# Mamba's first load by itself, and the sum of x and its norm on ScalarE instead of GpSimd

## The chip, the cores and the metric

The kernel runs on one core of a Trainium2 chip. The core has five engines that run their own instruction queues side by side: TensorE (PE) for matrix products, VectorE (DVE), ScalarE (ACT), GpSimd (POOL), and SyncE (SP), which here only issues transfers. PE, DVE, ACT and POOL wait for one another through semaphores. The metric is the device time of one launch in microseconds, as the median of several runs. One further execution is recorded by the profiler; its own time is a little different from the median, and both are given below.

## The reference, cut to what matters

The input `x` has 4 sequences of 1024 tokens with 256 features, all in float32. Four blocks follow one another:

```python
x = x + lora_attention(layernorm(x))
x = x + moe_ffn(layernorm(x))          # best 1 of 4 experts, weighted by its probability
h = layernorm(x)
x = x + (h + mamba2(h))                # the block that the change touches
x = x + moe_ffn(layernorm(x))          # same weights as the first FFN
```

The third block is the one to keep in mind. It needs `h` twice: as the input of Mamba's projections, and in the sum `x + h`, to which Mamba's result is added at the end. The norm has no learned scale or offset, so `h = x * rstd + shift`, with `rstd` one over the root of a token's variance (plus 1e-5) and `shift = -mean * rstd`, both one number per token.

Inside `mamba2`, a projection makes a gate `z` (512 features), the convolved part `xBC` (512 + 128 + 128) and eight step sizes `dt`. `xBC` passes through a causal convolution over 4 tokens and a SiLU; the state-space part runs over chunks of tokens; its result is gated, normed and projected back to 256 features.

## The kernel before, in words

Three phases follow one another in time. Attention, with some tiles of the first FFN woven in, ends near 1200 us; the other tiles of the first FFN end near 1406 us; Mamba runs from there to about 2110 us with tiles of the second FFN woven in; the tiles that remain of the second FFN end the run. The output of the first FFN lies in HBM as `x_mid`.

Mamba is cut into eight `Half` objects of 512 tokens each, `halves[0]` to `halves[7]`: first the first halves of the four sequences (`g == 0`), then the second ones (`g == 1`). A half has these steps, whose lines the profile names:

- `fetch` (L1195) loads its 512 x 256 tokens, 512 KB, into `xs`, of which there are three buffers. Half 0 is fetched on ACT's queue, half 1 on SP's, and half n + 2 on SP's at the end of half n's turn.
- `front` is a generator of 14 steps. The first is the norm in `layernorm`: statistics (L169, L172), `rstd` (L173 and `rsqrt`, L149 to L154), `shift` (L178), all on DVE, then four ACT activations (L180) that write `xln`. The second step transposes `xln` on PE (L190), copies the result to `xT` on ACT (L139), and adds `xln` to `xs` on POOL through `in_parts` (L1178, called at L1207). The third makes the step sizes (`softplus`, L1160 on). Six steps `channels(cc)` follow (L1210 to L1237), in the order 4, 5, 0, 1, 2, 3; then four gates (L1243), and the sums of step sizes.
- `channels` multiplies on PE (L1219), takes the last three tokens of the half before from `carry` into the head of the buffer `raw` on POOL (L1223), copies the product behind them on ACT (L1224), saves the last three tokens into `carry` on POOL when `g == 0` (L1226), makes the first tap on ACT (L1228), the three other taps on DVE (L1232), the tanh on ACT into `raw` (L1235), and the SiLU on DVE (L1236). `raw` has two buffers, so a channel waits for L1236 of the one two before it.
- `prepare(i)` and `chunk(i)` do the state-space part of 128 tokens: masks and decays (L1318 to L1325, with products on POOL), transposes of the channels (L1335 to L1348), and the state.
- `back` is a generator of eight steps: four of `project`, which writes x + h + Mamba's result to `rows` (L1409, L1410), then the FFN's norm, its transposes, the routing (L252 on), and last the ranks (L277 on) with four scattering DMAs that POOL issues (L310) into `sorted_rows`.
- The tiles of the second FFN start with `ffn_some`: a table made on DVE (L345 to L379), then on SP's queue the gather of the first tile's rows (L426) and its weights (L443, L450). A tile begins on PE with the transposes of these rows (L461).

What sets the order is `plan`, a table of four tuples per half: "f" is a step of the next half's front, "b" a step of the back of the half before, "t" a step of FFN tiles, "s" the start of new tiles, and a number that chunk of the present half. An engine's instructions follow from the order in which the program issues them, as priorities, but a planner that estimates when operands are ready may let an instruction pass another of its engine; `keep_in_program_order` pins an instruction behind the one that the program issued last on that engine. Only the first statistic of each norm in Mamba is pinned.

Of the kernel before, what the change touches and what calls it, by code (L numbers as in the profile page):

```python
# [38 lines left out]
AF = mybir.ActivationFunctionType  # L39
ALU = mybir.AluOpType  # L40
AX = mybir.AxisListType

P = 128
# [7 lines left out]
DIN, DST, DCONV, NMH, HD = 512, 128, 4, 8, 64  # L51
# [3 lines left out]
TB = 512  # L55
# [23 lines left out]
def hybrid_block(ctx: ExitStack, tc: tile.TileContext, t, out: bass.AP):  # L79
    nc = tc.nc  # L80
# [12 lines left out]
    def ps1(name):  # L93
        return psum_now["pool"].tile([P, 512], F32, tag="one", name=name, bufs=psum_now["one"])
# [48 lines left out]
    def rsqrt(v, name):  # L143

        n = v.shape[1]
        bits = keep.tile([P, n], I32, tag=f"rs_bits{n}", name=f"rs_bits_{name}", bufs=2)
        y = bits.bitcast(F32)
        u = keep.tile([P, n], F32, tag=f"rs_u{n}", name=f"rs_u_{name}", bufs=2)
        nc.vector.tensor_single_scalar(bits, v.bitcast(I32), 1, op=ALU.logical_shift_right)  # L149
        nc.vector.tensor_scalar(bits, bits, -1.0, float(0x5F3759DF), op0=ALU.mult, op1=ALU.add)  # L150
        for i in range(3):
            nc.vector.tensor_tensor(u, y, y, ALU.mult)
            nc.vector.scalar_tensor_tensor(u, u, -0.5, v, op0=ALU.mult, op1=ALU.mult)
            nc.vector.scalar_tensor_tensor(v if i == 2 else y, u, 1.5, y, op0=ALU.add, op1=ALU.mult)  # L154
# [6 lines left out]
    def layernorm(pool, xs, xln, name, pinned=False, beside=None):  # L161

        n = xs.shape[1]
        stats = pool.tile([P, n, 6], F32, tag="ln_stats", name=f"stats_{name}", bufs=2)
        mv = pool.tile([P, n, 2], F32, tag="ln_mv", name=f"mv_{name}", bufs=2)
        both = pool.tile([P, n + 4 * (beside is not None)], F32, tag=f"ln_rstd{beside is not None}", name=f"rstd_{name}", bufs=2)
        rstd = both[:, 0:n]
        for i in range(n):
            first = nc.vector.bn_stats(stats[:, i, :], xs[:, i, :])  # L169
            if pinned and i == 0:  # L170
                tc.keep_in_program_order(first)
            nc.vector.bn_aggr(mv[:, i, :], stats[:, i, :])  # L172
        nc.vector.tensor_single_scalar(rstd, mv[:, :, 1], EPS, op=ALU.add)  # L173
        if beside is not None:
            nc.vector.tensor_scalar(both[:, n:], beside, 1.0 / DIN, EPS, op0=ALU.mult, op1=ALU.add)
        rsqrt(both, name)
        shift = pool.tile([P, n], F32, tag="ln_shift", name=f"shift_{name}", bufs=2)
        nc.vector.scalar_tensor_tensor(shift, mv[:, :, 0], -1.0, rstd, op0=ALU.mult, op1=ALU.mult)  # L178
        for i in range(n):
            nc.scalar.activation(  # L180
                xln[:, i, :], xs[:, i, :], AF.Identity, bias=shift[:, i : i + 1], scale=rstd[:, i : i + 1]
            )
        return both[:, n:]

    def transposed(xln, dst, name):

        for k in range(2):
            pt = ps1(f"xT_{name}_{k}")
            for i in range(4):
                nc.tensor.transpose(pt[:, i * P : (i + 1) * P], xln[:, i, k * P : (k + 1) * P], ident)  # L190
            evacuate(k, dst[:, k, :], pt)
# [3 lines left out]
    x_mid = tc.dram_tile([NTOK, D], F32, name="x_mid")  # L195
# [26 lines left out]
    def small(shape, tag, name, dtype=F32, bufs=2):  # L222
        return keep.tile([P, *shape], dtype, tag=tag, name=f"{tag}_{name}", bufs=bufs)
# [18 lines left out]
    def send_parts(rows, tok0, name):  # L242
        xln = rows[:, :, 0:D]
        layernorm(keep, rows[:, :, D : 2 * D], xln, f"f{name}")
        yield
        xT = small([2, TB], "xT_r", name, bufs=1)
# [265 lines left out]
    def full_tiles(n, size=FT):  # L512

        return max(0, -(-(n - NE * (size - 1)) // size))
# [586 lines left out]
    pb = ctx.enter_context(tc.tile_pool(name="phase_b", bufs=1))  # L1101
    rows_from.update(pool=pb, bufs=1)

    def work(name, tag, bufs):
        return pb.tile([P, 512], F32, tag=tag, name=name, bufs=bufs)
# [69 lines left out]
    def in_parts(n, size, operands, op):  # L1175

        for i in range(0, n, size):
            nc.gpsimd.tensor_tensor(*operands(slice(i, i + size)), op)  # L1178
# [4 lines left out]
    class Half:  # L1183
# [8 lines left out]
        def fetch(self, queue=nc.sync):  # L1192
            name = self.name
            self.xs = pb.tile([P, 4, D], F32, tag="xs", name=f"xs_{name}", bufs=3)
            queue.dma_start(self.xs, x_mid[self.tok0 : self.tok0 + TB, :].rearrange("(n p) d -> p n d", p=P))  # L1195

        def load(self, past):
            name = self.name
            xln = pb.tile([P, 4, D], F32, tag="xln", name=f"xln_{name}")
            if past:  # L1200
                past.rstd = layernorm(pb, self.xs, xln, name, pinned=True, beside=past.sumsq)
            else:
                layernorm(pb, self.xs, xln, name, pinned=True)
            yield
            self.xT = pb.tile([P, 2, TB], F32, tag="xT_b", name=f"xT_{name}")
            transposed(xln, self.xT, name)
            in_parts(4, 1, lambda i: (self.xs[:, i], self.xs[:, i], xln[:, i]), ALU.add)  # L1207
            yield

        def channels(self, cc):  # L1210

            name = f"{self.name}_{cc}"
            if cc == 4 and self.g == 0:
                carries[self.b] = pb.tile([P, NCC, DCONV - 1], F32, tag="carry", name=f"carry_{self.b}", bufs=NB)
                nc.gpsimd.memset(carries[self.b], 0.0)
            carry = carries[self.b]
            pp = ps1(f"xbc_{name}")
            for k in range(2):
                nc.tensor.matmul(  # L1219
                    pp, w_in[:, k, DIN + cc * P : DIN + (cc + 1) * P], self.xT[:, k, :], start=(k == 0), stop=(k == 1)  # L1220
                )
            raw = pb.tile([P, DCONV - 1 + TB], F32, tag="xbc", name=f"raw_{name}", bufs=2)
            nc.gpsimd.tensor_copy(raw[:, 0 : DCONV - 1], carry[:, cc, :])  # L1223
            nc.scalar.copy(raw[:, DCONV - 1 :], pp)  # L1224
            if self.g == 0:
                nc.gpsimd.tensor_copy(carry[:, cc, :], raw[:, TB:])  # L1226
            acc = work(f"xc_{name}", "xc", 12)
            nc.scalar.activation(  # L1228
                acc, pp, AF.Identity, bias=conv_b[:, cc : cc + 1], scale=conv_w[:, cc, DCONV - 1 : DCONV]
            )  # L1230
            for k in range(DCONV - 1):
                nc.vector.scalar_tensor_tensor(  # L1232
                    acc, raw[:, k : k + TB], conv_w[:, cc, k : k + 1], acc, op0=ALU.mult, op1=ALU.add
                )
            nc.scalar.activation(raw[:, 0:TB], acc, AF.Tanh)  # L1235
            nc.vector.scalar_tensor_tensor(acc, raw[:, 0:TB], 1.0, acc, op0=ALU.add, op1=ALU.mult)  # L1236
            self.xc.append(acc)  # L1237
# [199 lines left out]
    halves = [Half(b, g) for g in range(2) for b in range(NB)]  # L1437
    evacuates.update(only_act=True)

    halves[0].fetch(nc.scalar)  # L1440
    halves[1].fetch()
    for _ in halves[0].front():
        pass
    halves[0].prepare(0)

    plan = (
        ("f", "b", "t", "b", "t", 0, "b", "t", "b", "t"),
        ("b", "f", "t", "f", "t", 1, "t", "f", "b", "f", "t"),
        ("b", "t", "f", "f", "t", 2, "f", "f", "b", "s", "t"),
        ("t", "f", "f", "t", "f", 3, "t", "f", "f"),  # L1450
    )
    y_out = out.rearrange("b s d -> (b s) d")
# [2 lines left out]
    for n, H in enumerate(halves):  # L1455
        after = halves[n + 1] if n + 1 < len(halves) else None
        front = after.front(halves[n - 1] if n else None) if after else iter(())
        for i in range(4):
            if i < 3:
                H.prepare(i + 1)  # L1460
            for step in plan[i]:
                if step == i:
                    H.chunk(i)
                elif step == "s":

                    n_tiles = full_tiles(n * TB, P) - n_done
                    n_done += n_tiles
                    if n_tiles:
                        coming = ffn_some(n_tiles, y_out, f"f2_{n}", 0 if after else n_tiles - 1)
                        next(coming)  # L1470
                else:
                    next({"b": back, "f": front, "t": tiles}[step], None)
            if i == 3 and after:
                after.prepare(0)

        if n + 2 < len(halves):
            halves[n + 2].fetch()
        tiles, back = chain(tiles, coming), H.back()
        coming = iter(())

# [70 lines left out]
```

## Time and profile before

| what | value |
|---|---|
| median of three runs | 2311.2 us (2309.44 to 2313.97) |
| profiled execution | 2317.05 us, its span 2315.3 us |
| mean granted TensorE clock | 0.949 of full speed |
| busy: PE, DVE, ACT, POOL | 2110.2, 1378.8, 867.1, 844.3 us |
| first loads of Mamba issued | 1410.05 us |
| first matmul of Mamba | 1421.42 us |
| POOL, adds of `xln` to `xs` (L1178) | 32 of 739 ns, 22.8 us in all |
| POOL, copies of three tokens (L1223, L1226) | 48 of 450 ns and 24 of 393 ns |
| ACT, activations of the same size as an add (L180) | 32 of 589 ns |

"Busy" is the time in which an engine executes something, over the whole span. The view by groups gives for each line of the code the number of instructions, the busy time, the mean of one, and the time that the engine stood idle before them with what ended it ("<-"). The timeline gives the start of each instruction or run of like instructions, its time, and in brackets the idle time before it. Durations and places all come from the one profiled execution.

### The profile page before, as it was taken

What the parts mean: (1) busy time and instruction counts of PE and PEld (TensorE: products, weight loads), DVE (VectorE), ACT (ScalarE), POOL (GpSimd) and SP (SyncE); (2) the same over time, 40 slices, a digit from 0 to 9 for tenths busy, and PEclk for the clock granted to TensorE, in tenths of its full rate; (3) what the DMA queues carried; (4) which work ended last, traced back from release to release, by engine and by line L of the source; (5) the groups of instructions that cost most, each with busy time, mean ns of one, the idle gap of its engine ahead of it and who ended that gap; (6) DMA issues with size and microseconds to landing.
All of it is one profiled execution on the core that took longest, in us unless ns stands there. A gap on an engine that the chain in (4) does not pass through costs nothing. (4 is left out here: it accounts for less than half of the span.)

```text
span 2315.3 us, 34722 instructions
## 1 busy us (share of the span) xinstructions
PE 2110.2 (91%) x12322; PEld 1472.2 (64%) x12322; DVE 1378.8 (60%) x3470; ACT 867.1 (37%) x1709; POOL 844.3 (36%) x1455
## 2 busy tenths in 40 slices
PE   5899999999999998989988997898799999999997
PEld 4444454554545555655566994566487877879987
DVE  5666666556655545565344334787967777775522
ACT  3365644445444443443411112453433433332210
POOL 3344433344443242341121111665635353443221
PEclk8799998999989999999999997899899999999999
DMA  9101011300131212132245683002153453544788
GB/s 332 36 21 50 22 36 51 102 29 24 40 121 67 86 44 81 35 115 87 88 164 186 221 320 108 0 10 89 65 204 136 138 194 125 181 162 142 273 317 304
DMA packets 148977, 278.19 MB, mean 120 GB/s; under 512 B 19965, under 2 KB 92031, under 8 KB 148801
## 3 DMA queue, kind: packets, MB, share of 16 engines
q1 hardware_dynamic: 120240, 227.45, 28.7%
q0 software_dynamic: 9920, 30.25, 3.6%
q10 hardware_dynamic: 18640, 18.23, 2.5%
q8 instruction: 100, 1.64, 0.3%
q14 instruction: 77, 0.62, 0.1%
HBM read 225.17 MB, written 51.12 MB: 119 GB/s over the span
## 5 line engine op out<-in xcount | busy, mean ns | idle before, releaser
L873 DVE TENSOR_REDUCE mx<-s 128x2 f32<-128x1024 f32 (+3 forms) x384 | 363.8, 953 | 86.6 <-PE s L864 80.6
L908 ACT ACTIVATE pe<-s 128x1024 f32<-128x1024 f32 (+3 forms) x384 | 309.0, 811 | 252.1 <-PE s L900 196.1
L919 PE MATMUL acc<-pe,v 128*32 128x512 f32 (+3 forms) x1536 | 263.1, 514 | 13.7 <-POOL pe L911 11.9
L911 POOL TENSOR_SCALAR_AFFINE_SELECT pe<-pe 128x256 f32<-128x256 f32 x256 | 104.4, 409 | 445.8 <-ACT pe L908 445.5
L476 PE MATMUL gu_f<-t_xT_f,t_Wg_f 128*128 128x128 f32 (+1 forms) x1216 | 236.1, 317 | 3.1 <-DVE t_xT_f L141 2.3
L476 PE MATMUL gu_f<-t_xT_f,t_Wu_f 128*128 128x128 f32 (+1 forms) x1216 | 229.9, 312 | 0.2
L872 DVE TENSOR_TENSOR s<-s,amats 128x256 f32<-128x256 f32 x256 | 109.2, 428 | 155.3 <-PE s L864 114.0
L476 PEld LDWEIGHTS gu_f<-t_xT_f,t_Wg_f 128*128 128x128 f32 x1216 | 183.3, 193 | 24.8 <-issue 6.4
L492 PE MATMUL y_f<-t_Wd_f,t_h_f 128*128 128x256 f32 x816 | 187.4, 383 | 7.6 <-DVE t_rows_f L499 2.8
L864 PE MATMUL s<-ks,qs 64*128 64x512 f32 (+3 forms) x768 | 172.8, 401 | 23.3 <-ACT pe L908 12.3
L476 PEld LDWEIGHTS gu_f<-t_xT_f,t_Wu_f 128*128 128x128 f32 x1216 | 184.9, 192 | 12.0 <-DMA t_Wu_f<-in_Wu 1.0
L900 PE MATMUL s<-qs,ks 64*128 64x512 f32 (+3 forms) x768 | 182.9, 441 | 10.0 <-DVE mx L873 7.4
L900 PEld LDWEIGHTS s<-qs,ks 64*128 64x128 f32 x768 | 80.0, 189 | 170.3 <-issue 95.4
L159 DVE SCALAR_TENSOR_TENSOR t_h_f<-t_h_f,gu_f 128x512 f32<-128x512 f32 x102 | 69.9, 686 | 193.5 <-ACT t_h_f L158 193.5
L492 PEld LDWEIGHTS y_f<-t_Wd_f,t_h_f 128*128 128x128 f32 x816 | 152.6, 191 | 38.0 <-issue 6.2
L158 ACT ACTIVATE t_h_f<-gu_f 128x512 f32<-128x512 f32 x102 | 60.9, 597 | 280.2 <-PE gu_f L476 280.1
L900 PE MATMUL s<-mneg,sel_r 64*128 64x512 f32 (+3 forms) x768 | 161.6, 367 | 0.0
L864 PEld LDWEIGHTS s<-ks,qs 64*128 64x128 f32 x768 | 85.0, 195 | 74.1 <-ACT pe L908 25.3
L1232 DVE SCALAR_TENSOR_TENSOR xc_m<-raw_m,conv_w,xc_m 128x512 f32<-128x512 f32 x144 | 111.4, 784 | 16.8 <-ACT xc_m L1228 14.9
L1178 POOL TENSOR_TENSOR m_m<-m_m,gm_m 128x256 f32<-128x256 f32 x128 | 93.8, 764 | 63.7 <-ACT gm_m L1325 62.7
L787 PE MATMUL qkv<-weff,xT 128*128 128x192 f32 x512 | 108.0, 357 | 7.7 <-ACT ks L838 4.3
L787 PEld LDWEIGHTS qkv<-weff,xT 128*128 128x128 f32 x512 | 87.8, 202 | 28.6 <-ACT ks L838 10.3
(450 smaller groups left out, 3912.9 us busy)
## 6 DMA issues: line engine op xcount, KB each, us to landing
t_Wg_f<-in_Wg SPq DMA_DIRECT2D x38, 1024.0 KB
t_Wu_f<-in_Wu SPq DMA_DIRECT2D x38, 1024.0 KB
t_Wd_f<-in_Wd SPq DMA_DIRECT2D x38, 1024.0 KB
sorted_rows<-blank SPq DMA_DIRECT2D x8, 2056.0 KB
t_Wg_f2p<-in_Wg SPq DMA_DIRECT2D x10, 1024.0 KB
t_Wu_f2p<-in_Wu SPq DMA_DIRECT2D x10, 1024.0 KB
t_Wd_f2p<-in_Wd SPq DMA_DIRECT2D x10, 1024.0 KB
t_Wg_f1p<-in_Wg SPq DMA_DIRECT2D x9, 1024.0 KB
```

What stands on the lines that cost most here:

```text
L476: nc.tensor.matmul(gu[:, i, j, :], w[which][:, k, f * P : (f + 1) * P], xT[:, k, :], start=(k == 0), stop=(k == 1))
L492: nc.tensor.matmul(y, hs[f // nf][:, f % nf, i * P : (i + 1) * P], wd[:, f, :], start=(f == 0), stop=(f == DFF // P - 1),)
L787: nc.tensor.matmul(pp[:, i, 0:192], B.xT[:, k, tok], B.weff[:, k, self.c * 192 : (self.c + 1) * 192], start=(k == 0), stop=(k == 1),)
L864: nc.tensor.matmul(sc[:, a, 0:w], self.q[p, qb // 4][r, qb % 4 * P : (qb % 4 + 1) * P], self.k[p, h][r, 0:w], start=True, stop=True,)
L872: nc.vector.tensor_tensor(sc[:, :, w - P : w], sc[:, :, w - P : w], bcast(amats, 1, 2), ALU.add)
L873: nc.vector.tensor_reduce(self.mx[:, qb, 2 * p : 2 * p + 2, h], sc[:, :, 0:w], axis=AX.X, op=ALU.max)
L900: nc.tensor.matmul(sc[:, a, off:512], sels[p][r, :] if part else self.k[p, kc // 4][r, kc % 4 * P : (kc % 4 + 1) * P], self.mneg[qt][r, of ...
L908: nc.scalar.activation(pe[:, :, off:512], sc[:, :, off:512], AF.Exp, scale=1.0 / math.sqrt(DK))
L911: nc.gpsimd.affine_select(diag, diag, [[0, 2], [1, P]], ALU.is_ge, 0.0, base=0, channel_multiplier=-1)
L919: nc.tensor.matmul(self.acc[32 * j : 32 * j + 32, off:512], self.v[:, kc, (DK + 1) * j : (DK + 1) * j + 32], pes[j // 2][:, j % 2, off:512 ...
L1178: nc.gpsimd.tensor_tensor(*operands(slice(i, i + size)), op)
L1232: nc.vector.scalar_tensor_tensor(acc, raw[:, k : k + TB], conv_w[:, cc, k : k + 1], acc, op0=ALU.mult, op1=ALU.add)
```

## The change

Five things are changed.

1. `fetch` of half 0 goes to SP's queue and is issued alone. Half 1 is fetched on ACT's queue once the first front step of half 0 (its norm, with the four activations) has been issued; half 2 on ACT's queue at the end of half 0's turn; all later ones on SP's as before. A fetch on ACT's queue is pinned in ACT's order.
2. `layernorm` returns `rstd`, `shift` and what it returned before.
3. The sum `x + h` is made on ACT in place, as `xs * (rstd + 1) + shift`, in four activations behind the transposes and their copies. DVE makes `rstd + 1` once per half (`one_more`, 128x4). The four POOL adds of each half are gone.
4. The two copies of three tokens in `channels` go from POOL to ACT.
5. In the third tuple of `plan`, the last "f" (the channel with `cc == 3`) is issued behind the last "b" (ranks and scatters) and "s", instead of ahead of them.

```diff
@@ layernorm
-        return both[:, n:]
+        return rstd, shift, both[:, n:]
@@ Half.fetch
-            queue.dma_start(self.xs, x_mid[self.tok0 : self.tok0 + TB, :].rearrange("(n p) d -> p n d", p=P))
+            load = queue.dma_start(self.xs, x_mid[self.tok0 : self.tok0 + TB, :].rearrange("(n p) d -> p n d", p=P))
+            if queue is nc.scalar:
+                tc.keep_in_program_order(load)
@@ Half.load
+            rstd, shift, roots = layernorm(pb, self.xs, xln, name, pinned=True, beside=past.sumsq if past else None)
             if past:
-                past.rstd = layernorm(pb, self.xs, xln, name, pinned=True, beside=past.sumsq)
-            else:
-                layernorm(pb, self.xs, xln, name, pinned=True)
+                past.rstd = roots
+            one_more = small([4], "one_more", name)
+            nc.vector.tensor_single_scalar(one_more, rstd, 1.0, op=ALU.add)
             yield
             self.xT = pb.tile([P, 2, TB], F32, tag="xT_b", name=f"xT_{name}")
             transposed(xln, self.xT, name)
-            in_parts(4, 1, lambda i: (self.xs[:, i], self.xs[:, i], xln[:, i]), ALU.add)
+
+            for i in range(4):
+                nc.scalar.activation(
+                    self.xs[:, i, :], self.xs[:, i, :], AF.Identity, bias=shift[:, i : i + 1], scale=one_more[:, i : i + 1]
+                )
             yield
@@ Half.channels
-            nc.gpsimd.tensor_copy(raw[:, 0 : DCONV - 1], carry[:, cc, :])
+            nc.scalar.copy(raw[:, 0 : DCONV - 1], carry[:, cc, :])
             nc.scalar.copy(raw[:, DCONV - 1 :], pp)
             if self.g == 0:
-                nc.gpsimd.tensor_copy(carry[:, cc, :], raw[:, TB:])
+                nc.scalar.copy(carry[:, cc, :], raw[:, TB:])
@@ phase b
-    halves[0].fetch(nc.scalar)
-    halves[1].fetch()
-    for _ in halves[0].front():
-        pass
+    halves[0].fetch()
+    for i, _ in enumerate(halves[0].front()):
+        if i == 0:
+            halves[1].fetch(nc.scalar)
     halves[0].prepare(0)
...
-        ("b", "t", "f", "f", "t", 2, "f", "f", "b", "s", "t"),
+        ("b", "t", "f", "f", "t", 2, "f", "b", "s", "f", "t"),
...
-            halves[n + 2].fetch()
+            halves[n + 2].fetch(nc.sync if n else nc.scalar)
```

## The prediction, made before the result was known

> **What bounds the kernel now.** I read the page's engine totals and its forty slices first.
>
> ```profile
> PE 2110.2 (91%) x12322; PEld 1472.2 (64%) x12322; DVE 1378.8 (60%) x3470; ACT 867.1 (37%) x1709; POOL 844.3 (36%) x1455
> PE   5899999999999998989988997898799999999997
> DVE  5666666556655545565344334787967777775522
> PEclk8799998999989999999999997899899999999999
> ```
>
> TensorE is busy 91% of the span, so only places where it idles or runs at a lower clock can be bought. The change touches Mamba alone (1406 to 2110 us), and there the digits fall in slices 25 to 29. The view by stretches opens them; the columns are length, then busy time of PE, PEld, DVE, ACT and POOL, granted clock, DMA share and GB/s.
>
> ```profile
> 1406.30:1421.40 15.10, 0.00 (x0) 0.00 (x0) 5.13 (x28) 0.64 (x2) 1.01 (x1) 0.58 0.36 110
> 1421.40:1433.00 11.60, 11.12 (x31) 6.96 (x32) 2.45 (x11) 4.01 (x8) 2.96 (x5) 0.51 0.00 0
> 1433.00:1456.00 23.00, 19.03 (x56) 9.23 (x55) 22.48 (x45) 14.02 (x28) 6.63 (x12) 0.94 0.00 1
> 1456.00:1500.00 44.00, 39.58 (x137) 24.23 (x137) 31.73 (x67) 17.58 (x33) 34.71 (x52) 0.80 0.00 0
> 1500.00:1550.00 50.00, 46.11 (x225) 32.72 (x223) 43.88 (x109) 27.54 (x58) 29.30 (x44) 0.93 0.04 11
> 1550.00:1600.00 50.00, 40.30 (x163) 25.25 (x164) 46.76 (x120) 21.09 (x44) 35.86 (x51) 0.90 0.25 90
> 1650.00:1679.00 29.00, 20.20 (x78) 13.21 (x77) 26.86 (x86) 10.11 (x22) 18.05 (x26) 0.76 0.37 134
> 1700.00:1800.00 100.00, 96.88 (x591) 78.31 (x590) 75.12 (x195) 38.05 (x78) 44.99 (x69) 1.00 0.46 158
> ```
>
> The reader is to see three regimes. The first 15 us hold no matmul: Mamba waits for its first x. Up to 1679 VectorE is nearly full (22.48 of 23, 46.76 of 50, 26.86 of 29) with half-clock patches. From 1679 on TensorE is full. I then read the waits of TensorE in those stretches, by time.
>
> ```profile
> 1410.05 0.93 SPq L1195 DMA_DIRECT2D xs_m<-x_mid  x2
> 1410.05 0.45 ACTq L1195 DMA_DIRECT2D xs_m<-x_mid  x1
> 1415.77 0.75 DVE L169 BATCH_NORM_STATS2 stats_m<-xs_m 128x6 f32<-128x256 f32 x2 [8.91 <-DMA xs_m<-x_mid]
> 1421.42 2.17 PE L190 MATMUL xT_m<-mats,xln_m 128*128 128x128 f32 x8 [15.14 <-ACT xln_m L180]
> ...
> 1588.44 0.66 PE L461 MATMUL xT_f<-mats,t_rows_f 128*128 128x128 f32 x2 [2.88 <-DMA t_rows_f<-sorted_rows]
> 1672.61 0.66 PE L461 MATMUL xT_f<-mats,t_rows_f 128*128 128x128 f32 x2 [5.17 <-DMA t_rows_f<-sorted_rows]
> ```
>
> The last two are the first FFN tiles of halves 1 and 2, held by their gather. Last, the groups that the change takes from POOL, and what ACT and POOL wait for between 1420 and 1700 (total, times, longest).
>
> ```profile
> L1178 POOL TENSOR_TENSOR xs_m<-xs_m,xln_m 128x256 f32<-128x256 f32 x32 | 22.8, 739 | 20.5 <-ACT xln_m L180 20.5
> L1223 POOL COPY raw_m<-carry 128x3 f32<-128x3 f32 x48 | 21.6, 450 | 122.6 <-DVE xc_m L1236 115.0 <-DVE place_m L297 5.8 <-DVE sp_p_m L1168 1.7
> L180 ACT ACTIVATE xln_m<-xs_m,shift_m,rstd_m 128x256 f32<-128x256 f32 x32 | 16.6, 589 | 48.4 <-DVE shift_m L178 48.4
> ...
> POOL raw_m L1223 <- DVE xc_m L1236: 26.6, 13, 3.4
> ...
> ACT raw_m L1224 <- DVE xc_m L1236: 10.9, 7, 3.6
> ```
>
> **The change, part by part.** The sum is made against the profiled execution, 2317.05 us (span 2315.3 and 1.75 around it). That is 5.85 above the median of the runs, 2311.2, so differences are carried over to 2311.2.
>
> *A. The first load.* Today three loads of 512 KB start at 1410.05, one on ACT's queue, two on SP's. The last packet of half 0's comes 5.18 us after issue and the first statistics at 5.72. The lone loads of this trace (1534.91 and 1616.22, on SP) take 3.41 and 3.46 to the last packet: 1.77 less. Of the statistics, only a half's first is pinned; three of half 1's run at present inside half 0's norm (1415.77 to 1420.73, six foreign instructions). With half 1's load issued behind half 0's norm they can't: −0.75. Together 2.5 us earlier. How much survives? The clock record has half speed from 1408.9 to 1432.8, with its changes on a grid of 3.41 us, and the xbc matmuls run without a break from 1429.19. The Trainium skill ("TensorE: Matmul & The Clock Gate", What's actually happening) has the clock at half or full, raised after one busy window of some 3.4 us that runs freely. It speaks against the change: if the rise stays at 1432.8, a start 2.5 us earlier buys 2.5 us of half-speed work, worth 1.25 at full speed; if it comes one window earlier, 2.5 + 1.7 are gained. The row says that after 1433 VectorE is what is full (22.48 of 23), so that matrix time is only partly the price. By the row −2.5, by the rule −1.25; I take −1.8. Range −3.3 to +0.5 (the SP queue could be as slow as ACT's). Half 1's load is issued on ACT some 8 us later and needed at 1457, over 30 us after: hidden.
>
> *B. Half 1's norm.* It now holds three statistics of half 2 (1457 to 1459), and half 2's load isn't there yet after the change: 3 × 0.41, less overlap, −1.0 (−1.4 to 0). Their work comes later, at 1518, as a part of C.
>
> *C. Half 2's load on ACT's queue*, pinned behind the last activity of half 1's first preparation (the bt copy, 1512.6 to 1515.2). By A's two durations it lands 3.9 to 5.7 later, 1516.6 to 1521; VectorE wants it at 1518.66. A stall of 0 to 2.3, and what is late next is all of VectorE's queue; the cover is its 2.30 us wait for a mo product at 1531. The first statistic is pinned, so nothing passes it. +0.9 (0 to +2.5). The issue itself costs ACT 0.45.
>
> *D. The sums and small copies.* Off POOL: 32 adds (22.8) and 72 copies of 128x3 (21.6 + 9.4). Onto ACT: 32 activations at 0.587 (the form of L180), 18.8, and 72 copies. No row has a 128x3 copy on ACT; the nearest are 128x128 at 0.263 and 128x512 at 0.585, a straight line through which gives an estimate of 0.16, so 11.5 in all. Onto VectorE: eight `one_more`, at L173's 0.485, 3.9. The activations' cover: ACT idles 5.6, 5.4 and 5.1 us behind the xT copies of halves 0 to 2, waiting for the step sizes, and four take 2.0. Were they placed ahead of these copies, each half would lose up to 0.5 per activation. `one_more` stands beside the norm's own tail, with VectorE's wait for the next product; without that cover +3.9. The small copies lengthen each channel's chain L1236, L1224, L1228, L1232 by 0.16 to 0.32 instead of a POOL hop: some twenty channels lie before 1679, +3 to +4.5 uncovered, about half of it met by ACT's idle time: +1.5. Against it, tanh no longer waits for POOL's carry (three times, 3.6 us): −1.5. What of VectorE's relief? The skill ("SBUF — State Buffer", SBUF: two separate sides) says that VectorE and GpSimd lock one pair of ports, and the later one blocks for a whole instruction. By that rule 32 adds gone are worth up to 22.8 us of VectorE. The trace doesn't agree: of some 76 us by which VectorE's instructions in Mamba exceed the usual time of their forms, 0.3 end with an xs add and none with a small copy (34.8 end with POOL's m products, which stay). I take the trace. Sum of D: 0 (−3 to +4.5).
>
> *E. The plan.* The last channel of a front (2 matmuls, 3 activations, 3 × 0.784 + about 0.7 = 3.1 us of VectorE) goes behind the last step of the back (rank matmuls L277, VectorE's slots, four scatters on POOL's queue) and behind `s` (steering on VectorE, then gather L426 and weights L443, L450 on SP's queue). So scatters and gather can come up to 3.1 earlier, against stalls of 2.88 (half 1) and 5.17 (half 2): at most −6.0. Against: POOL must still finish its scatters (1659.94 to 1665.36) and VectorE cast the steering row (L370, 1666.02 to 1668.93) before the gather at 1669.82; and the moved channel is late for the xh transposes L1335, which have 3.8 us of cover at half 2 (its L1236 ends at 1654.85, they start at 1658.69). If that cover is gone, +3. Half 0 has no tiles then; from half 3 on TensorE is full and the gather is hidden. I take half: −3.0 (−8 to +3).
>
> *F. From 1700 on* TensorE is idle some 3 us in 100, on ACT's gm, bt and yT copies. ACT gets 2.0 to 3.5 us more per half at 38% busy: 0 (−3 to +4).
>
> Sum: −1.8 − 1.0 + 0.9 + 0 − 3.0 + 0 = **−4.9**. Profiled 2312.15, median **2306.3 us**. Some 0.2%, 4.6 us, is what a measurement of this kernel can tell from no change; the forecast lies just beyond it.
>
> **The rivals.** *Only the start counts* (R1). VectorE is as full up to 1679 as before (26.86 of 29), so a gather that comes earlier only moves the wait to its products. Then A and B alone remain, partly: −2, 2309. For it: the full VectorE. Against it: 5.17 us in which TensorE waits for a DMA alone.
>
> *The gather's stalls go whole* (R2): −8, one window of half clock less after one of them (half speed at 1582.9 and 1664.9) −3.4, and A and B, less C: −13, 2298. Against it: it needs both gathers more than 3.1 us earlier.
>
> *ACT inherits POOL's waits* (R3, slower). A small copy into `raw` needs its buffer free (L1236), but no matmul; placed where POOL had it, it stands at the head of ACT's queue, and behind it the tanh, exp, xh and m activations, for which VectorE and TensorE wait. POOL waited 26.6 us there, ACT 10.9 for the same release; the difference, 15.7, becomes ACT's. VectorE is busy 85% from 1433 to 1679, so 13.4 of it arrives: −4.9 + 13.4 = +8.5, 2319.7. It cancels the gain from 4.9 and is slower beyond telling from 9.5. Against it: L1224 follows at once and waits for the same release today.
>
> **How the numbers follow.** Forecast 0.40, R2 0.14, R1 0.19, R3 0.27. The forecast's own range, 2302 to 2310, lies two thirds on the faster side: faster 0.26 + 0.14 = 0.40; same 0.14 + 0.19 = 0.33; slower 0.27. Leaving out half of R2 and of R3 gives 2298 to 2320.
>
> **What would show it.** A: first statistics at 4 us after issue, not 5.7, and only four inside the norm; the clock's rise at 1432.8 or one window off. C: VectorE's wait for xs near 1518. D: the small copy near 0.16, ACT's wait for L1236 still near 11 and not 26; four in-place activations behind the xT copies. E: waits of L461 for t_rows below 2.9 and 5.2, with L1335 not waiting longer for L1236. The prediction is wrong if the written order of the instructions shifts elsewhere: only few are pinned, and a small edit can reorder VectorE's queue in every half.

## The result, and the profile after

The changed kernel is slower: 2329.84 us median of 20 runs against 2315.04 us for the kernel before in the same comparison, a ratio of 1.0065 with a 95% interval of 1.0051 to 1.0079, or +15 us (11.8 to 18.3). On the 2311.2 us of the prediction that is 2326, above the range of 2298 to 2320, on the other side from the forecast.

The profiled execution of the changed kernel took 2320.1 us, only 4.8 more than the one of before. That difference misleads. The first load of Mamba was issued at 1410.05 us before and at 1400.47 after, though the work up to there has the same instructions, in almost the same order: attention and the first FFN were 9.6 us shorter in that one execution, with a mean granted clock of 0.96 instead of 0.95. So the two traces are compared here from the first load (L1195) on. From it to the first rank product (L277) of half 6, which lies near the end of Mamba, the kernel before took 726.8 us and the changed one 739.7. This stretch is called the Mamba stretch below.

The page's totals and slices after the change:

```profile
PE 2106.7 (91%) x12322; PEld 1470.6 (63%) x12322; DVE 1383.9 (60%) x3478; ACT 891.5 (38%) x1813; POOL 790.6 (34%) x1351
PE   5899999999999998989988996888899999999997
DVE  5666666556655455655244336787967777785422
PEclk9699998999989999999999997889999999999999
```

POOL lost 53.7 us of work, as costed (53.8), ACT gained 24.4 where 30.3 was costed, and TensorE has the same number of instructions. In the Mamba stretch TensorE is idle for 66.8 us instead of 59.9, and busy for 673.0 instead of 666.9 with the same 3700 matmuls: idle time is about half of the 12.9 us, and the rest is matmuls that last longer. Which of these met a lower clock was not split. The view by stretches, with every stretch set 9.57 us earlier so that both kernels count from their first load (columns as before: length, PE, PEld, DVE, ACT, POOL, clock, DMA share, GB/s):

```profile
1396.73:1411.83 15.10, 2.16 (x8) 1.16 (x8) 4.45 (x23) 2.57 (x6) 1.00 (x1) 0.67 0.19 65
1411.83:1423.43 11.60, 11.45 (x27) 6.85 (x28) 4.21 (x18) 4.94 (x12) 0.00 (x0) 0.55 0.03 10
1423.43:1446.43 23.00, 17.52 (x52) 8.24 (x51) 21.69 (x43) 13.71 (x36) 0.19 (x1) 0.92 0.00 1
1490.43:1540.43 50.00, 42.91 (x195) 29.79 (x196) 41.60 (x92) 23.14 (x53) 24.30 (x34) 0.93 0.07 21
1640.43:1669.43 29.00, 24.53 (x95) 13.22 (x93) 27.33 (x83) 13.04 (x35) 13.10 (x16) 0.97 0.10 37
1690.43:1790.43 100.00, 96.37 (x585) 77.78 (x584) 74.66 (x193) 40.32 (x85) 39.35 (x58) 1.00 0.45 158
```

The first stretch now holds matmuls (2.16 us against 0): the start is earlier. In the fourth row TensorE has 195 matmuls in 50 us where it had 225 before, and VectorE is less busy too, 41.60 against 43.88. That is where half 0's last products and half 2's norm lie. The timeline of the start:

```profile
1400.47 0.38 SPq L1195 DMA_DIRECT2D xs_m<-x_mid  x1
1404.33 0.75 DVE L169 BATCH_NORM_STATS2 stats_m<-xs_m 128x6 f32<-128x256 f32 x2 [7.04 <-DMA xs_m<-x_mid]
1408.50 0.16 DVE L178 SCALAR_TENSOR_TENSOR shift_m<-mv_m,rstd_m 128x4 f32<-128x4 f32 x1
1408.86 0.38 ACTq L1195 DMA_DIRECT2D xs_m<-x_mid  x1
1412.73 0.43 DVE L169 BATCH_NORM_STATS2 stats_m<-xs_m 128x6 f32<-128x256 f32 x1 [3.99 <-DMA xs_m<-x_mid]
```

In the kernel before, the same shift was here:

```profile
1420.57 0.16 DVE L178 SCALAR_TENSOR_TENSOR shift_m<-mv_m,rstd_m 128x4 f32<-128x4 f32 x1
```

The first statistics after the change come 3.86 us after issue (5.72 before) and the first shift 8.03 after it (10.52 before). These 2.49 us are the gain that was forecast.

Counted from the first shift, the last row of half 0's result (L1410, now L1417) comes 11.0 us later than before. About 5.5 of them have come together step by step before the place that is shown next; part of these may come from where the clock is at half speed: the kernel e12 below, with the order of before, is 2.8 us late at the same place for that reason. The other 5.5 arise here, at half 2's norm beside half 0's last products. `yT` is the transposed result of half 0 that the mo products need. First the kernel before:

```profile
1514.82 1.10 PE L1403 MATMUL yT_m<-mats,z_m 128*128 128x128 f32 x4
1515.96 0.59 ACT L139 COPY yT_m<-yT_m 128x512 f32<-128x512 f32 x1 [0.45 <-PE yT_m L1403]
1518.66 0.42 DVE L169 BATCH_NORM_STATS2 stats_m<-xs_m 128x6 f32<-128x256 f32 x1
1523.30 0.59 ACT L139 COPY yT_m<-yT_m 128x512 f32<-128x512 f32 x1
1525.10 0.47 DVE L1410 SCALAR_TENSOR_TENSOR rows_m<-mo_m,rstd_m,xs_m 128x256 f32<-128x256 f32 x1
1525.21 2.08 ACT L180 ACTIVATE xln_m<-xs_m,shift_m,rstd_m 128x256 f32<-128x256 f32 x4 [1.32 <-DVE shift_m L178]
1527.74 0.48 DVE L1410 SCALAR_TENSOR_TENSOR rows_m<-mo_m,rstd_m,xs_m 128x256 f32<-128x256 f32 x1
```

And the changed kernel:

```profile
1512.56 0.73 DVE L169 BATCH_NORM_STATS2 stats_m<-xs_m 128x6 f32<-128x256 f32 x2
1513.30 0.38 DVE L169 BATCH_NORM_STATS2 stats_m<-xs_m 128x6 f32<-128x256 f32 x1
1513.69 0.38 DVE L169 BATCH_NORM_STATS2 stats_m<-xs_m 128x6 f32<-128x256 f32 x1
1514.51 0.38 PE L1410 MATMUL yT_m<-mats,z_m 128*128 128x128 f32 x2
1515.63 0.58 ACT L139 COPY yT_m<-yT_m 128x512 f32<-128x512 f32 x1
1521.01 0.48 DVE L1417 SCALAR_TENSOR_TENSOR rows_m<-mo_m,rstd_m,xs_m 128x256 f32<-128x256 f32 x1
1521.05 2.07 ACT L180 ACTIVATE xln_m<-xs_m,shift_m,rstd_m 128x256 f32<-128x256 f32 x4 [4.85 <-DVE shift_m L178]
1523.03 0.56 ACT L139 COPY yT_m<-yT_m 128x512 f32<-128x512 f32 x1
1526.53 0.48 DVE L1417 SCALAR_TENSOR_TENSOR rows_m<-mo_m,rstd_m,xs_m 128x256 f32<-128x256 f32 x1 [2.46 <-PE mo_m L1416]
```

Three queues have another order. On VectorE, four statistics stand in half 2's norm where one did, so its root starts later. On TensorE, the four transposes of the first yT ran together; now two run at 1509.01 and two at 1514.51, behind eight products of the decays (L1318 and L1319, now L1325 and L1326). On ACT, two copies of yT stood ahead of half 2's four xln activations. After, only one does. The second stands behind them, and they wait 4.85 us for half 2's shift. The second row of half 0's result comes 5.52 us after the first instead of 2.64.

### The profile page after: what moved, and what is told of

Same layout as the page of the kernel before. It is cut to its first block, busy times and chain, and to the rows that moved or that the text cites. A ratio compares the mean times of both kernels' runs of the same rounds, so it can differ in the third digit from the quotient of the medians.

```text
span 2320.1 us, 34629 instructions
## 1 busy us (share of the span) xinstructions
PE 2106.7 (91%) x12322; PEld 1470.6 (63%) x12322; DVE 1383.9 (60%) x3478; ACT 891.5 (38%) x1813; POOL 790.6 (34%) x1351
## 5 line engine op out<-in xcount | busy, mean ns | idle before, releaser
L919 PE MATMUL acc<-pe,v 128*32 128x512 f32 (+3 forms) x1536 | 261.5, 513 | 14.0 <-POOL pe L911 11.6
L476 PEld LDWEIGHTS gu_f<-t_xT_f,t_Wg_f 128*128 128x128 f32 x1216 | 183.1, 193 | 31.0 <-issue 11.8
L476 PEld LDWEIGHTS gu_f<-t_xT_f,t_Wu_f 128*128 128x128 f32 x1216 | 185.7, 193 | 11.8 <-DMA t_Wu_f<-in_Wu 0.8
L1239 DVE SCALAR_TENSOR_TENSOR xc_m<-raw_m,conv_w,xc_m 128x512 f32<-128x512 f32 x144 | 112.6, 790 | 13.7 <-ACT xc_m L1235 12.5
L787 PEld LDWEIGHTS qkv<-weff,xT 128*128 128x128 f32 x512 | 86.9, 200 | 29.9 <-ACT ks L838 11.6
```

What stands on the lines that cost most here:

```text
L476: nc.tensor.matmul(gu[:, i, j, :], w[which][:, k, f * P : (f + 1) * P], xT[:, k, :], start=(k == 0), stop=(k == 1))
L787: nc.tensor.matmul(pp[:, i, 0:192], B.xT[:, k, tok], B.weff[:, k, self.c * 192 : (self.c + 1) * 192], start=(k == 0), stop=(k == 1),)
L919: nc.tensor.matmul(self.acc[32 * j : 32 * j + 32, off:512], self.v[:, kc, (DK + 1) * j : (DK + 1) * j + 32], pes[j // 2][:, j % 2, off:512 ...
L1239: nc.vector.scalar_tensor_tensor(acc, raw[:, k : k + TB], conv_w[:, cc, k : k + 1], acc, op0=ALU.mult, op1=ALU.add)
```

## The experiments

The sizes come from two measures: the ratio of times with its interval, and the Mamba stretch in one trace. The second has a limit. One kernel (e4 and e12 are the same) took 724.7 and 729.7 us in two executions. The record of TensorE's granted clock shows windows of half speed on a grid of 3.41 us, called clock windows here, and the two executions had the grid at different places in the program; the last section has the figures. Differences of a few us in the stretch count only between traces whose grids lie alike; the ratios decide elsewhere.

| kernel | what it has | Mamba stretch, us | ratio to before, 95% interval |
|---|---|---|---|
| before | | 726.8 | |
| after | all | 739.7 | 1.0065 (1.0051 to 1.0079) |
| e1 | fetches alone | 734.1 | 1.0025 (1.0007 to 1.0042) |
| e2 | sums on ACT alone | 734.6 | 1.0016 (1.0000 to 1.0032) |
| e3 | small copies on ACT alone | 729.2 | 0.9995 (0.9977 to 1.0013) |
| e4 | plan alone | 724.7 | 0.9983 (0.9962 to 1.0005) |
| e5 | e1, half 2's load early | 727.0 | 0.9997 (0.9977 to 1.0017) |
| e6 | after, half 2's load early | 728.6 | 1.0011 (0.9995 to 1.0026) |
| e7 | e2, sums issued at the gates | 733.8 | 1.0028 (0.9999 to 1.0056) |
| e8 | plan, loads as e5 | 724.8 | 0.9983 (0.9966 to 1.0000) |
| e9 | e7, sums pinned there | 734.7 | 1.0013 (0.9994 to 1.0031) |
| e10 | e5, half 2's statistics pinned | 731.0 | 1.0001 (0.9980 to 1.0022) |
| e11 | e8 with the sums of e9 | 728.4 | 0.9997 (0.9974 to 1.0021) |
| e12 | plan alone, again | 729.7 | 1.0002 (0.9985 to 1.0019) |

**The four parts by themselves.** The parts of the diff above, one at a time, put into the kernel before. Two theories were stated: L, half 2's late load costs; A, ACT's longer queue costs.

> The changed fetches alone (half 0 by itself on SP, half 1 and half 2 on ACT's queue); sums and small copies stay on POOL, the plan is the old one. Theory L (the late load of half 2 puts all four of its statistics inside its norm, and what waits for that norm comes late): 2.5 us gained up to the first shift, 5 to 8 lost between it and half 0's last mo product, so +3 to +6 us against the kernel before. Theory A (ScalarE's longer queue is what costs): -1 to -3 us, only the start's gain.

> The sums of x and its norm on ScalarE in place, alone. Theory A: the activations stand ahead of copies of xT and yT in ScalarE's queue, +5 to +10 us, most of it before the fourth half. Theory L: within 2 us of the kernel before.

> The two copies of three tokens on ScalarE, alone. Theory A: the first channels' chain is longer, +2 to +5 us, seen already at half 0's xh transposes. Theory L: within 2 us of the kernel before.

> The last channel behind the ranks and the start of the tiles, alone. By the step of the prediction -3 us (-8 to +3), with shorter waits of L461 for the gathered rows of halves 1 and 2. Both theories, A and L, leave it near 0; a third one (the plan itself costs) says +3 to +8.

The fetches alone cost 0.25%, 5.8 us (1.6 to 9.7): as theory L says, and against A. The sums alone cost 0.16%, 3.7 us (0 to 7.4), less than A's +5 to +10, and more than L's "within 2", though the interval reaches into both. The small copies cost nothing that can be measured, against A. So each theory has one part. The sum of the four ratios is +0.19%, some 4 us, where the whole change costs 15. With e12 for e4 it is +0.38%, some 9 us; four intervals of some 4 us each way leave either sum uncertain by about 8.

The small copies are instructive: the slower rival of the prediction came true in the waits and not in the time. Waits of ACT for the buffer `raw`, 1406 to 1700 us, kernel after and then e3 (total, times, longest):

```profile
ACT raw_m L1230 <- DVE xc_m L1243: 24.5, 19, 3.7
```

```profile
ACT raw_m L1223 <- DVE xc_m L1236: 19.2, 15, 3.0
```

POOL waited 26.6 us for this release before, and ACT now waits for nearly as long, against its 10.9 before. Yet e3 is at 0.9995. So most of the waiting moved to ACT, which is 38% busy, and delayed nothing that shows in the time.

**Half 2's load.** In e5 and e6 half 2 is fetched on ACT directly behind half 1, near the start, instead of at the end of half 0's turn (the lines in which e6 differs from the changed kernel, and e5 in the same way from e1; "..." marks what is left out):

```diff
         if i == 0:
             halves[1].fetch(nc.scalar)
+            halves[2].fetch(nc.scalar)
...
-        if n + 2 < len(halves):
-            halves[n + 2].fetch(nc.sync if n else nc.scalar)
+        if n and n + 2 < len(halves):
+            halves[n + 2].fetch()
```

> The changed fetches alone, but half 2 is fetched on ScalarE's queue directly behind half 1, near the start, instead of at the end of half 0's turn. Theory L2 (half 2's late load costs, since its statistics then all lie inside its norm, and half 0's last products wait for that norm): the lag that the changed fetches show between half 0's second chunk and its last mo product (3.5 to 9.2 us after the first shift) is gone, 3 to 4 remain there, and the whole is within 2 us of the kernel before. Rival (any load not issued at once costs, half 1's above all): the lag stays at 8 to 10 us.

> The whole change, with half 2 fetched directly behind half 1. Theory L2: 4 to 7 us faster than the changed kernel, so 8 to 11 us above the kernel before. Rival (the late load costs only where POOL has the sums): as the changed kernel, +15 us.

Both went as theory L2 says, e6 further than it said. e5 takes 7.1 us out of e1's Mamba stretch (734.1 to 727.0; the grids of the two lie within 0.13 us of each other), and its ratio falls from 1.0025 to 0.9997. By the ratios that is 6.5 us, with an interval of some 6 each way. e6 takes the whole change from 1.0065 to 1.0011, some 12.5 us of the 15 (about 8 to 17), and its interval holds no change. In e6's trace the order is that of before again:

```profile
1513.46 0.59 ACT L139 COPY yT_m<-yT_m 128x512 f32<-128x512 f32 x1
1516.62 0.42 DVE L169 BATCH_NORM_STATS2 stats_m<-xs_m 128x6 f32<-128x256 f32 x1
1518.74 0.59 ACT L139 COPY yT_m<-yT_m 128x512 f32<-128x512 f32 x1
1525.05 0.48 DVE L1417 SCALAR_TENSOR_TENSOR rows_m<-mo_m,rstd_m,xs_m 128x256 f32<-128x256 f32 x1
1525.10 2.08 ACT L180 ACTIVATE xln_m<-xs_m,shift_m,rstd_m 128x256 f32<-128x256 f32 x4 [5.77 <-DVE shift_m L178]
1527.86 0.47 DVE L1417 SCALAR_TENSOR_TENSOR rows_m<-mo_m,rstd_m,xs_m 128x256 f32<-128x256 f32 x1
```

One statistic in half 2's norm, two copies of yT ahead of the xln activations, and rows 2.81 us apart. The four transposes of the first yT stand together too. They do in every kernel here but the changed one and e1, the two with the late load.

Was it the load or the statistics that the late load drags into the norm? In e10 the load is early and the four statistics are pinned, so that they stay together:

```diff
-            if pinned and i == 0:
+            if pinned and (i == 0 or name == "m2_0"):
```

> As e5 (the changed fetches with half 2's load early), but all four statistics of half 2 are pinned, so that none of them runs ahead inside half 1's norm. Theory S (it is the place of these statistics, inside half 2's norm, that costs, not the load): the lag at half 0's last mo product goes from 3.4 back to 7 to 10 us. Rival Q (it is the late DMA in ScalarE's queue, or the time of its landing): the lag stays at 2.5 to 4.5.

Neither fits. Counted from the first shift, half 0's last row comes 3.4 us later than before in e5, 6.6 in e10 and 9.2 in e1, all three with grids that lie alike. The 3.4 us are no price of e5's loads: e12, whose instructions up to there are those of before and whose windows up to there are those of e5, has them too, and each matmul of e5 up to that row is within 0.04 us of e12's. Against e12, then, e5 loses nothing by this row, e10 3.2 us and e1 5.8.

The four statistics make the root of half 2's norm start 2.0 us later than in e12 in e10, and 2.2 in e1. What follows differs. In e10 three VectorE instructions of the chunk stand inside the root (L1378, L1390 and L1391 of its kernel), and it ends 5.6 us later than in e12; but the copies of yT keep their place. In e1 none stands inside it, and it ends 3.5 us later; but the copy of the first yT comes 6.6 us later than in e12 (0.7 in e10), behind the decays, and the second stands behind the xln activations. So the statistics in the norm are a part of e1's loss, some 2 us directly; what each of the other two orders is worth was not tried by itself. In time e10 is at 1.0001, so its 3 us are within what the ratio can't tell.

**The sums on ACT.** The trace of e2 loses in small steps where TensorE is full: 1.5, 1.9 and 1.9 us up to the last rows of halves 3, 4 and 5. Here is the first, beside half 5's norm, before and then in e2:

```profile
1784.35 0.56 ACT L139 COPY yT_m<-yT_m 128x512 f32<-128x512 f32 x1
1784.81 0.59 ACT L158 ACTIVATE t_h_f<-gu_f 128x512 f32<-128x512 f32 x1
1785.43 0.69 DVE L159 SCALAR_TENSOR_TENSOR t_h_f<-t_h_f,gu_f 128x512 f32<-128x512 f32 x1 [2.03 <-ACT t_h_f L158]
```

```profile
1787.31 0.56 ACT L139 COPY yT_m<-yT_m 128x512 f32<-128x512 f32 x1
1787.78 1.58 ACT L1210 ACTIVATE xs_m<-xs_m,shift_m,one_more_m 128x256 f32<-128x256 f32 x3
1789.26 0.57 ACT L158 ACTIVATE t_h_f<-gu_f 128x512 f32<-128x512 f32 x1
1789.87 0.69 DVE L159 SCALAR_TENSOR_TENSOR t_h_f<-t_h_f,gu_f 128x512 f32<-128x512 f32 x1 [3.43 <-ACT t_h_f L158]
```

Three sums stand ahead of a tile's tanh, VectorE waits 3.43 us for it instead of 2.03, and the `yoff` product behind it holds the next yT transposes on TensorE. So e7 issues each sum behind a gate, later in the program, in place of the block in `load`, and e9 adds the pin of the last line but one (cut to the gates):

```diff
             for i in range(4):
                 self.gate(i)
+                added = nc.scalar.activation(self.xs[:, i, :], self.xs[:, i, :], AF.Identity,
+                    bias=self.shift[:, i : i + 1], scale=self.one_more[:, i : i + 1])
+                tc.keep_in_program_order(added)
                 yield
```

> The sums on ScalarE alone, one behind each of the four gates instead of all four behind the copies of xT. Theory A1 (their place in ScalarE's queue costs: ahead of the tanh of a tile and of copies of yT): the steps of 1.5 to 2 us in each of halves 3 to 5 are gone, and the lag at half 6's ranks falls from 7.8 to 0 to 4 us. Rival (ScalarE's added work costs wherever it stands): still 7 to 9 us.

> The sums on ScalarE alone, one behind each gate and now pinned there; the kernel with the unpinned ones (e7) had them still right behind a copy of yT, three ahead of a tile's tanh. Theory A1 (the place in ScalarE's queue): the steps of 1.5 to 2 us in halves 3 to 5 are gone, the lag at half 6's ranks falls from 7.1 to between -1 and 3. Rival (ScalarE's added work, or POOL's m products that no longer stand behind the sums): the steps stay, 6 to 8 us.

e7 told nothing on the place: the planner put the sums exactly where they had been (the wait is 3.43 us again), presumably because they were ready there. In e9 they are gone from there:

```profile
1782.38 0.56 ACT L139 COPY yT_m<-yT_m 128x512 f32<-128x512 f32 x1
1782.85 0.59 ACT L158 ACTIVATE t_h_f<-gu_f 128x512 f32<-128x512 f32 x1
1783.47 0.69 DVE L159 SCALAR_TENSOR_TENSOR t_h_f<-t_h_f,gu_f 128x512 f32<-128x512 f32 x1 [1.96 <-ACT t_h_f L158]
```

The tanh follows the copy at once, and the three steps shrink from 5.4 to 2.3 us together. But the total does not fall, 734.7 us: e9 loses 7 us by half 2 where e2 loses 3.5, in a half 1 whose norm now takes 12.9 us from `rstd` to `shift` against 9.6 before, with the same seven foreign VectorE instructions inside it in another order. That the steps shrink where the sums have left speaks for their place as the cause; that the sums on ACT could be free in another place is not shown. By time, e9 (1.0013) can't be told from e2 (1.0016) nor from no change.

**Put together.** e8 has the new plan and the early loads of e5; e11 adds e9's sums; e12 measures the plan again.

> The new plan and the first load by itself, halves 1 and 2 both behind half 0's norm; sums and small copies on POOL. If the parts add: -2 (plan) and 0 to -2 (loads), so -2 to -5 us against the kernel before. Rival (new orders of the queues each time, so that parts do not add): anywhere from -5 to +5.

> The new plan, half 0's load by itself with halves 1 and 2 behind its norm, the sums on ScalarE pinned behind the gates, small copies on POOL. If both mended parts are worth what the theories say: load to half 6's ranks 720 to 726 us (726.8 before, 739.7 in the changed kernel), so -1 to -7 us against the kernel before. Rival (each new order of the queues costs something of its own): +2 to +6.

> The new plan alone once more, timed longer, since its first interval (0.9962 to 1.0005) leaves open whether this part is a gain. By the trace of e4 (2.1 us less up to half 6's ranks) -2 us, ratio 0.999; by the step of the prediction -3 us, ratio 0.9987; if it only looked so, 1.000 or above.

e8 is at 0.9983 with an interval that touches 1: possibly 4 us faster than before, and clearly faster than the changed kernel (1.0065). Its grid of clock windows lies within 0.02 us of that of e6, which has the sums and small copies on ACT beside the same loads and plan: 724.8 us against 728.6. That is 3.8 us for sums and copies, as the 3.7 of e2. e11 is at 0.9997: the mended sums gain nothing. e12 takes away what e4 had promised; the two intervals together leave the plan within a few us of no change. None of these is shown to beat the kernel before.

## Why the prediction was wrong, point by point

*A, the first load*: the gain was right, 2.49 us to the first shift against 2.5 forecast. How much of it survives the half clock (1.8 taken, 1.25 by the rule, 2.5 by the row) stays open. At the first xbc products 0.8 went back in the changed kernel and 1.2 in e1, where half clock lasts until 13.8 and 14.7 us after the first shift against 12.2 before. But in e6, e8 and e11 it ends at 11.5 to 11.9 us and nothing went back, while e12, with the loads of before, is 1.2 late at the same place (half clock until 14.5 us). It is the position of the windows that decides there, and that differs from execution to execution; a match with one of the three figures would be luck. Half 1's load on ACT landed in time as stated.

*B, half 1's norm without half 2's statistics, −1.0*: wrong. The three statistics left it, but it became longer, 10.67 us against 9.56 from `rstd` to `shift` (9.31 in e1). Three VectorE instructions of the chunk stand inside it before and after, and in the changed kernel VectorE waits there 2.1 us for TensorE's products, against 0.8 before.

*C, half 2's load on ACT*: **the step that failed**, +0.9 (0 to +2.5) stated, and some 12.5 us measured in the whole change (e6 against it), 7.1 alone (e5 against e1). Its working asked only whether the load lands before VectorE wants it. It did: it was issued at 1506.4, the statistics began at 1512.56, and VectorE had no gap of more than 0.04 us in the five before them. What costs is the order that comes with a late load. Statistics that had long been done came into the norm, decays came between the transposes of yT on TensorE, and the second copy of yT fell behind the xln activations that wait for this norm, while half 0's rows wait for norm and copy. That the late load costs is shown by e5 and e6; the share of each of these three orders is not. The step named "all of VectorE's queue" as late next, and looked neither at ACT's queue, which has the xln activations of this norm in it, nor at TensorE's. By its own size, 11.6 us, this term is more than half of the 20 by which the sum missed. That half 0's `rstd` comes out of half 2's norm (the argument `beside`) was in the code.

*D, the sums and copies, 0*: right for the copies, which are even shorter in their queue than estimated (192 ns each, but 0.09 us apart from the next). Their uncovered cost, stated as +3 to +4.5, should have been 3.2 to 6.4 (twenty channels at 0.16 to 0.32); e3 shows none of it. The term was too low for the sums: 3.7 us by the ratio. The text had the price ("up to 0.5 per activation" where they stand ahead of a copy), and three of them ahead of a tanh cost 1.5 us in half 5, but it took the cover of halves 0 to 2 for all eight. The trace's verdict on VectorE's relief held: the eight norms of Mamba take 53.3 us from `rstd` to `shift` before and 53.1 after (58.0 in e6), with 32 POOL adds gone.

*E, the plan, −3.0*: the first half of the mechanism is right, the gain is not there. TensorE no longer waits for the gathered rows: 8.1 us before, none in e4 and after. But the ratios, 0.9983 and 1.0002, show no gain that holds. TensorE waits elsewhere instead. Its two longest waits in e4 from 1550 to 1710 us, which were 2.9 and 1.1 us before:

```profile
PE csl_m L1318 <- DVE by_s L1288: 5.3, 2, 3.1
PE mo_m L1409 <- ACT yT_m L139: 5.1, 2, 2.7
```

A third, 3.4 us of xbc products for L1380, is new: the three are 9.8 us longer together, for the 8.1 that went. In e4, counted from the first shift, half 0's ranks come 2.4 us earlier and half 1's last row 2.9 later. That is rival R1's outcome, a wait that only moves, and not by the moved channel: the xh transposes wait 3.6 us for L1236 as before (3.5). e4 has two more half-speed windows in the stretch, 88.7 us against 81.9; whether the earlier gather brings them is not shown.

*F, the full stretches, 0 (−3 to +4)*: too low in the same way as D; the steps of e2, 5.4 us in its trace, lie here.

*The slower rival* had the right sign with the wrong mechanism: its waits came, its price did not (e3).

*Left open*: the parts add to some 4 to 9 us, the whole costs 15; half 2's late load costs some 12.5 in the whole and some 7 alone. This points to parts that make each other worse, but the intervals, about 8 each way for the sum and 5 to 6 for the two prices, don't settle it. Through which of the reordered instructions was not tried.

## What to carry to other kernels

Where a planner orders the queues, the price of a later transfer is not its wait but the order that it brings: follow every consumer that it drags along, and what these consumers stand ahead of on each engine, above all on those that finish the work of the part before. To move an instruction later in the program is no experiment unless it also moves in its queue; pin it, and read the queue first. And before two traces are compared, set them to a common event near the change, see that their clock windows lie alike from there, and measure one kernel twice.

## What the runs showed of the hardware

*The position of the clock windows was worth up to 5 us.* One kernel (e4, e12) took 724.7 and 729.7 us for the same Mamba stretch. TensorE's half-speed windows begin and end on a grid of 3.41 us, whose place in the program differs between executions: from the first shift they begin at 32.6, 42.9 and 53.1 us in e4, and at 35.0 and 48.7 in e12. Between the two traces the lag of e12 grows almost only where one has half clock and the other hasn't: 1.2 us at the first xbc products, 2.0 between 50 and 64 us, 1.7 by 132 us, of which 3.0 are given back by 145 us, where e4 meets a window. Pairs whose windows lie alike show how little else differs. From the first shift to the last mo products of half 0, where e12 is 3.5 us behind e4, every matmul of e4 lies within 0.1 us of the kernel before (windows within 0.06 us), and every one of e5 within 0.04 us of e12 (windows within 0.02).

*VectorE's small instructions fall into POOL's pace.* The instructions of a norm's root take 0.16 us alone, and 0.65 while POOL's m products run. From the kernel before, in half 0 with POOL idle and in half 5 with POOL busy:

```profile
1418.99 0.16 DVE L153 SCALAR_TENSOR_TENSOR rs_u_m<-rs_u_m,rstd_m 128x4 f32<-128x4 f32 x1
...
1779.34 2.78 POOL L1178 TENSOR_TENSOR m_m<-m_m,gm_m 128x256 f32<-128x256 f32 x4
1779.43 0.65 DVE L154 SCALAR_TENSOR_TENSOR rs_bits_m<-rs_u_m,rs_bits_m 128x8 f32<-128x8 f32 x1
1780.12 0.65 DVE L152 TENSOR_TENSOR rs_u_m<-rs_bits_m 128x8 f32<-128x8 f32 x1
```

One follows each POOL product, at its pace of 0.69 us. In halves 6 and 7 all 13 instructions from `rstd` to `shift` are slow (0.45 to 0.66 us each), and what takes 2.5 us alone (half 0 of the changed kernel) takes 8.2. That is how the lock that the prediction weighed would look; the traces show the pace, not the ports. It comes with the m products and the other products on POOL beside the norm, which no part of the change removes.
